# Attention's constants loaded during layer norm, the one-hot products turned round, and late projections stored by ScalarE's queue

## The chip, the cores and the metric

The kernel runs on one core of a Trainium2 chip. A core has five engines that work at the same time, each through its own instructions in order: PE (TensorE, matrix products into PSUM), DVE (VectorE), ACT (ScalarE), POOL (GpSimd) and SP (SyncE, which here only issues DMAs). DMAs are issued from the queues of SP, ACT and POOL and are carried out by 16 DMA engines that all three share. An engine stands still while its next instruction waits for a semaphore, whatever is queued behind that instruction.

The metric is the device time of one execution in microseconds. One execution has been profiled as well; times below are counted from the start of its span.

## What is computed

The input x has 2 x 2048 tokens of 256 numbers. Cut to what matters:

```python
xn = (x - mean(x)) / sqrt(var(x) + 1e-5)              # layer norm
q, k, v = xn @ W.T + b                                # 16 heads of 16
rpk, rpv = rel_k[idx], rel_v[idx]                     # idx = clip(key - query, -128, 128) + 128
w = softmax((q @ k.T + q . rpk) / 4)
s = ((w @ v + w . rpv) as rows) @ Wo.T + bo           # attention with relative positions
e = argmax(xn @ Wg + bg)                              # one of 8 experts for a token
g = silu(gelu(xn @ W1[e]) @ W2[e])                    # 256 -> 1024 -> 256
out = x + s * g
```

All of it is float32.

## The kernel before, in words

The work is done in stages, one behind the other on PE.

**Layer norm, up to about 58 us.** Eight blocks of 512 tokens. `take_stats(i)` takes the mean and variance of a block on DVE and the root on ACT; `normalise(i)` scales the block on DVE (`xn`, L249), stores it in `xn_d` by SP for the experts, and turns it on PE (`tps`, L259), ACT copying the result into `xnT`. `logits(i)` multiplies by Wg (`plog`, L267). The loop takes the statistics of block i + 1 before it normalises block i. Between the blocks, `work_pieces(n)` puts in the next n of a list of 28 pieces: query, key and value projections of the first half of the tokens (`queries`, `keys`, `right_rows`, `values_of`). Their results go to DRAM (`q_d`, `k_d`, `qx_d`, `v_d`) by SP. A piece `values_of` adds the bias to `vt` on DVE (L326); two tiles `vt`, preset to one by POOL (L390), are used in turn.

**Routing, from 58 to about 125 us.** DVE counts the tokens of each expert by one-hot tables and gives every token a slot in a list in which each expert's tokens fill whole tiles of 256. To turn the list round (which token is in which slot), 32 matrix products add up over blocks of 128 tokens: `atplace` (128 x 128, one-hot of the place in a block of slots) and `inblock` (128 x 46, the token's number at its block of slots) give `ptok` (128 places x 46 blocks), copied to `token`. In the profile each float32 product is two passes, so these are 64. POOL then gathers the tokens of the first two tiles (`get_tokens`), SP loads the weights of their experts (`get_weights`: a value load of the expert's number, then W1 and W2, 1 MB each), and POOL loads attention's constants: `wo_t`, `bo_t`, `relk_t`, `rvd`, `rvc`, `ones_r`. DVE presets the key tiles `kT` from `ones_r` (L542) and builds `into` from `rvc` (L546); PE multiplies `into` by each group of `wo_t` and DVE adds that to `wo_t` (L551, L554), here called the fold. The last value pieces stand around this.

**Experts, from 125 to about 397 us.** 19 tiles of 256 tokens (`work`): PE turns the tokens (`xp`), multiplies by W1 (`hp`), ACT takes gelu, PE multiplies by W2 (`yp`), and the result is stored by ACT's queue (`ys_d`).

**Attention, from 397 us to the end.** 128 chunks: a loop over n takes a chunk of 128 queries of four heads. Its scores against nearby keys, the band, take a way of their own: `rel_scores` (L855) and `to_keys` send the relative scores through DRAM (`qr_d`, then back as `r`) on SP; `band_scores` (L893) adds them; `band_weights` takes exponentials on ACT (L926) and sends the weights through DRAM (`w_d`, back as `wr`) on POOL. Four chunks make a unit, whose far keys are taken by `far_scores` (L1048, exponentials L1058) and `far_values` (L1068). Each n has about five steps; the functions put down by `at(k, ...)` are issued behind step k. Within these, the first four n also do the query, key and value projections of the second half of the tokens, which `load_late` prepares: it loads the weights, the bias `bvl` and the turned tokens `sacc` (from `xT_d`) by ACT's queue and adds a constant to `bvl` on DVE (L711). `late_rows` (L729, L735), `late_right` (L744) and `late_values` (L759, L767) are these pieces. Each stores its result by SP at once; the pool of the late `vt` tiles has two buffers, preset by POOL (L754).

The order in each of the stages is written out by hand. Instructions of a later stage can nevertheless stand between those of an earlier one in an engine's queue: POOL's first memsets of L754 run at 88.6 us.

Of the kernel before, what the change touches and what calls it, by code (L numbers as in the profile page):

```python
# [34 lines left out]
def attn_moe_gate_kernel(  # L35
# [137 lines left out]
    with ExitStack() as own:  # L173
# [172 lines left out]
        def work_pieces(n):  # L346
            for what, *args in pieces[:n]:
                what(*args)
            del pieces[:n]

        take_stats(0)
        for i in range(NI):
            if i + 6 < NI:
                get_x(i + 6)
            if i + 1 < NI:
                take_stats(i + 1)
            normalise(i)
            if i == 0:
                nc.vector.tensor_scalar(bq_t, bq_t, HD**-0.5, None, ALU.mult)
                nc.vector.tensor_scalar(bk_t, bk_t, rkc[:, 0:1], None, ALU.add)  # L360

                nc.vector.tensor_tensor(
                    right, rkc[:, 1:2].to_broadcast([P, HEADS]),
                    rkc[:, 0:1].to_broadcast([P, HEADS]), ALU.subtract,
                )
# [15 lines left out]
                nc.gpsimd.memset(ones, 1.0)  # L381
                nc.gpsimd.memset(zq, 0.0)
                nc.gpsimd.iota(
                    begin, pattern=[[TE, NE]], base=0, channel_multiplier=0,
                    allow_small_or_imprecise_dtypes=True,
                )
                nc.gpsimd.iota(place, pattern=[[1, P]], base=0, channel_multiplier=0)
                nc.gpsimd.iota(number, pattern=[[P, NT]], base=0, channel_multiplier=1)
                for vt in vts:
                    nc.gpsimd.memset(vt, 1.0)  # L390
                for n in range(NI):
                    nc.sync.dma_start(out=qx_heads[:, 0, n * TB : (n + 1) * TB], in_=zq)
            if i == 1:
                nc.vector.tensor_tensor(
                    bvl, bvl, rve[:, 0:1, :].to_broadcast([P, HEADS, HD]), ALU.add
                )
            if i > 0:
                logits(i - 1)
                work_pieces(1)
            if i > NL:  # L400
                n = i - 1 - NL
                nc.sync.dma_start(
                    out=xT_d[n * P : (n + 1) * P, :].rearrange("p (k t) -> p k t", k=ND),
                    in_=xnT[:, :, (i - 1) * TB : i * TB],
                )
        logits(NI - 1)
        work_pieces(1)
        nc.sync.dma_start(
# [83 lines left out]
        ptok = lnps.tile([P, NB], F32, name="tps")  # L492
        for i in range(NI):
            ts = slice(i * CB, (i + 1) * CB)
            nc.vector.tensor_tensor(
# [14 lines left out]
        nc.vector.tensor_reduce(expf, over, AX.X, ALU.add)  # L510
        nc.vector.tensor_scalar(expert, expf[:, :, 0], float(E - 1), None, ALU.min)
        nc.vector.tensor_copy(filled, ends[:, E - 1 : E])
        work_pieces(13)
        for t in range(NT):
            nc.tensor.matmul(
                ptok, lhsT=atplace[:, t, :], rhs=inblock[:, t, :], start=(t == 0),
                stop=(t == NT - 1),
            )
        nc.vector.tensor_copy(token, ptok)
        inputs = [get_tokens(i, feed) for i in range(2)]  # L520
        weights = [get_weights(i, feed) for i in range(2)]


        wo_t = load("wo_t", [P, NG, D], wo.rearrange("(g p) m -> p g m", p=P))
        bo_t = load("bo_t", [P, D], bo.partition_broadcast(P))
        relk_t = load("relk_t", [P, TB], relk)
        rvd = load("rvd", [P, 2, HD], relv.rearrange("(a p) d -> p a d", p=P))
        rvc = load("rvc", [P, 2], relv_cols)
        ones_r = load("ones_r", [P, 1], ones_rows)
        nc.gpsimd.memset(zeros, 0.0)  # L530
        into = tables.tile([P, HG, 32], F32, name="into")
        nc.gpsimd.memset(into, 0.0)
        for t in q_homes:
            nc.gpsimd.memset(t, 0.0)
        nc.gpsimd.memset(stat, LOW)
# [2 lines left out]
        for z in shifts:  # L538
            nc.gpsimd.memset(z, 0.0)
        work_pieces(len(pieces) - 2)  # L540
        for t in k_homes:
            nc.vector.tensor_copy(t, ones_r.to_broadcast([P, S]))  # L542

        nc.vector.tensor_tensor(vdiff, rvc[:, 1:2], rvc[:, 0:1], ALU.subtract)
        for j in range(HG):
            nc.vector.tensor_copy(  # L546
                into[32 * j : 32 * j + 32, j, MASS : MASS + 1], vdiff[32 * j : 32 * j + 32, :]
            )
        for g in range(NG):
            ps = lnps.tile([P, D], F32, name="tps")  # L550
            nc.tensor.matmul(  # L551
                ps, lhsT=into.rearrange("p j i -> p (j i)"), rhs=wo_t[:, g, :], start=True, stop=True
            )
            nc.vector.tensor_tensor(wo_t[:, g, :], ps, wo_t[:, g, :], ALU.add)  # L554

        nc.vector.tensor_copy(rel0, relk_t[:, 0:1])
        nc.vector.tensor_scalar(relk_t, relk_t, rel0, None, ALU.subtract)
        nc.vector.tensor_tensor(rvd, rvd, rve[:, 0:1, :].to_broadcast([P, 2, HD]), ALU.subtract)
# [86 lines left out]
    def _attention(own, again):  # L645
# [59 lines left out]
        def load_late():  # L705
            tiles = [outp.tile([P, ND, D], F32, name=n) for n in ("gt", "gt", "xo", "xo")]
            for t, w in zip(tiles, (wq, wk, wv)):
                nc.scalar.dma_start(out=t, in_=w.rearrange("(k p) m -> p k m", p=P))
            bvl = tiles[3][:, 0, :].rearrange("p (h x) -> p h x", x=HD)
            nc.scalar.dma_start(out=bvl, in_=bv.partition_broadcast(P))  # L710
            nc.vector.tensor_tensor(  # L711
                bvl, bvl, rve[:, 0:1, :].to_broadcast([P, HEADS, HD]), ALU.add
            )
# [7 lines left out]
            late["w"], late["bvl"], late["xT"] = tiles[:3], bvl, xT  # L721

        def late_rows(i, n, a):

# [8 lines left out]
            t = exps.tile([P, TB], F32, name="ex")  # L733
            bias, scale, dst = ((bq_t, HD**-0.5, q_d), (bk_t, 1.0, k_d))[n]
            nc.scalar.activation(t, ps, AF.Identity, bias=bias[:, a : a + 1], scale=scale)  # L735
            nc.sync.dma_start(out=dst[a * P : (a + 1) * P, cols], in_=t)
            if n == 0:
                lateq[i, a] = t

        def late_right(i):  # L740
            cols = slice((NL + i) * TB, (NL + i + 1) * TB)
            ps = sps.tile([P, TB], F32, name="sp")
            for a in range(ND):
                nc.tensor.matmul(  # L744
                    ps[:HEADS, :], lhsT=rights[a], rhs=lateq.pop((i, a)), start=(a == 0),
                    stop=(a == ND - 1),
                )
            rt = exps.tile([P, TB], F32, name="ex")
            nc.scalar.copy(rt[:HEADS, :], ps[:HEADS, :])
            nc.sync.dma_start(out=qx_heads[:, 1, cols], in_=rt[:HEADS, :])  # L750

        def late_values(i, half):
            vt = vtp.tile([P, NG, 2, HG, VW], F32, name="vt")
            nc.gpsimd.memset(vt, 1.0)  # L754
            ps = sps.tile([P, 2, NG, HG, HD], F32, name="sp")
            for c in range(2):
                t0 = (2 * half + c) * P
# [8 lines left out]
            for c in range(2):  # L766
# [3 lines left out]
                    late["bvl"].rearrange("p (g j) x -> p g j x", j=HG),  # L770
                    ALU.add,
                )
            w = HG * VW
            n = NL + i
            nc.sync.dma_start(
                out=v_d[n * P : (n + 1) * P, :].rearrange("p (g c w) -> p g c w", c=CB, w=w)[
                    :, :, 2 * half : 2 * half + 2, :
                ],
                in_=vt.rearrange("p g c j x -> p g c (j x)"),
            )  # L780

        late_pieces = []
        for i in range(NI - NL):
# [413 lines left out]
        while n < NCH or values or any(queues) or n <= NCH + 2 * CB + 1:  # L1197
# [180 lines left out]
```

## Time and profile before

| what | value |
|---|---|
| time, median of 3 runs | 2311.96 us (2306.64 to 2318.05) |
| the profiled execution's own time | 2312.8 us |
| its span, first to last instruction | 2311.1 us |
| PE busy | 2205.3 us (95%) |
| ACT busy | 1295.6 us (56%) |
| DVE busy | 1063.1 us (46%) |
| POOL busy | 443.2 us (19%) |
| moved by DMA | 488.31 MB, mean 211 GB/s |
| layer norm and routing, until the experts' first turn | 0 to 124.7 us |
| experts | 124.7 to 396.9 us |
| attention | 396.9 us to the end |

How to read the rows. A row of the timeline or of a group has the engine, the line of the kernel, the operation, what it writes and reads, their shapes and the count; in the timeline the start and the time from first to last end stand ahead, and in square brackets the idle time of that engine before it and what ended it. PEld is PE's loading of weights, which overlaps its products. PEclk is the clock that PE was granted. A busy PE need not be PE at full speed, because its ends are modelled, so half clock shows in PEclk and in the duration of a pass rather than in the busy share. A window's row has the time that each engine was busy in a stretch, with its instructions, and after them the granted clock, the busy share of the 16 DMA engines and the rate.

### The profile page before, as it was taken

To read this page: it belongs to the slowest core of one execution; us is meant where nothing else is said; L and a number is where in the kernel's file an instruction comes from. 1 tells how busy PE (TensorE), PEld (TensorE's weight loads), DVE (VectorE), ACT (ScalarE), POOL (GpSimd) and SP (SyncE) were. 2 spreads that over 40 slices of the span, in tenths; PEclk is the share of its full clock that TensorE was granted. 3 is DMA by queue.
4 is the path that set the end of the run, shared out by engine and by line. 5 is a ranking of instruction groups with operands and counts; after the bars stand their busy time and mean duration, and the time that the engine had idled before them with its cause. 6 is when DMAs were issued, how large, how long until landed. Compare 5 with 4: busy or idle time off the path is not lost. (4 is left out here: it accounts for less than half of the span.)

```text
span 2311.1 us, 58525 instructions
## 1 busy us (share of the span) xinstructions
PE 2205.3 (95%) x24314; PEld 1432.7 (62%) x24314; DVE 1063.1 (46%) x2689; ACT 1295.6 (56%) x2543; POOL 443.2 (19%) x643
## 2 busy tenths in 40 slices
PE   7899999899999999999999999999999999999997
PEld 5588887455666556656565555566666656566653
DVE  5410000245555455555455444455555555555542
ACT  2111111237777666767666566666666666666764
POOL 1211110011333333321111222211111111111221
PEclk9899999899999999999999999999999999999999
DMA  6565553677777667776676666666756676666652
GB/s 204 206 190 187 187 185 106 226 230 233 237 243 244 212 221 232 245 236 206 205 234 210 231 231 220 213 213 227 224 198 216 221 222 223 200 208 213 233 195 85
DMA packets 256534, 488.31 MB, mean 211 GB/s; under 512 B 17120, under 2 KB 204672, under 8 KB 255744
## 3 DMA queue, kind: packets, MB, share of 16 engines
q1 hardware_dynamic: 207840, 297.31, 39.6%
q0 software_dynamic: 41008, 178.84, 23.1%
q10 hardware_dynamic: 7408, 8.27, 1.1%
q8 instruction: 196, 3.21, 0.6%
q14 instruction: 82, 0.67, 0.1%
HBM read 247.91 MB, written 236.45 MB: 210 GB/s over the span
## 5 line engine op out<-in xcount | busy, mean ns | idle before, releaser
L1058 ACT ACTIVATE ex<-sp 128x512 f32<-128x512 f32 x1728 | 892.7, 587 | 535.7 <-PE sp L1048 412.4
L1048 PE MATMUL sp<-qh,kT 32*128 32x512 f32 (+7 forms) x4096 | 767.1, 560 | 19.3 <-DVE stat L903 19.2
L903 DVE CUSTOM_DVE_ANT_0 r<-sp,r 128x384 f32<-128x384 f32 (+1 forms) x512 | 275.5, 538 | 594.1 <-PE sp L1048 327.3
L893 PE MATMUL sp<-kT,qh 31*128 31x384 f32 (+1 forms) x1024 | 453.6, 523 | 0.0
L1048 PEld LDWEIGHTS sp<-qh,kT 31*128 31x128 f32 (+1 forms) x4096 | 298.0, 184 | 207.0 <-issue 136.1
L1068 PE MATMUL av<-ex,v 128*17 128x256 f32 (+2 forms) x7168 | 423.0, 371 | 0.0
L1068 PEld LDWEIGHTS av<-ex,v 128*17 128x17 f32 (+1 forms) x7168 | 195.3, 99 | 176.6 <-issue 69.0
L855 PE MATMUL sp<-relk_t,qh 32*128 32x256 f32 x1024 | 289.1, 404 | 12.0 <-DVE qr L864 9.4
L926 ACT ACTIVATE r<-r,shift 128x384 f32<-128x384 f32 (+1 forms) x512 | 283.2, 614 | 0.0
L969 DVE COPY wt<-mp 128x512 f32<-128x512 f32 x368 | 242.4, 684 | 11.2 <-PE mp L967 6.2
L967 PEld LDWEIGHTS mp<-ident,r 128*128 128x128 f32 x1472 | 156.3, 141 | 141.3 <-issue 130.2
L941 POOL DMA_DIRECT2D wr<-w_d x128 | 97.4, 761 | 704.6 <-PE sp L1048 168.4
L967 PE MATMUL mp<-ident,r 128*128 128x128 f32 x1472 | 217.0, 282 | 2.1 <-DVE wt L969 2.1
L864 DVE COPY qr<-sp 128x512 f32<-128x512 f32 x256 | 175.2, 685 | 41.9 <-PE sp L1048 32.6
L855 PEld LDWEIGHTS sp<-relk_t,qh 32*128 32x128 f32 x1024 | 169.9, 185 | 26.4 <-DVE qr L864 9.8
L990 PE MATMUL mp<-ident,wr 128*128 128x128 f32 x1024 | 158.1, 278 | 25.7 <-DMA wr<-w_d 15.2
L939 POOL DMA_DIRECT2D w_d<-r x128 | 72.7, 568 | 532.5 <-ACT r L926 525.2
L607 ACT ACTIVATE hT<-hp 128x512 f32<-128x512 f32 x76 | 45.3, 597 | 215.7 <-PE hp L600 215.7
L893 PEld LDWEIGHTS sp<-kT,qh 31*128 31x128 f32 x1024 | 150.4, 184 | 8.9 <-issue 5.7
L990 PEld LDWEIGHTS mp<-ident,wr 128*128 128x128 f32 x1024 | 120.3, 142 | 46.3 <-DVE qh L953 22.5
L600 PE MATMUL hp<-xsT,w_t 128*128 128x256 f32 x608 | 134.4, 379 | 1.0 <-DVE xsT L586 1.0
L615 PE MATMUL yp<-w_t,hT 128*128 128x256 f32 x608 | 134.4, 379 | 0.0
(189 smaller groups left out, 2023.9 us busy)
## 6 DMA issues: line engine op xcount, KB each, us to landing
qr_d<-qr SPq DMA_DIRECT2D x128, 768.0 KB
r<-qr_d SPq DMA_DIRECT2D x128, 768.0 KB
w_d<-r POOLq DMA_DIRECT2D x128, 768.0 KB, 5.0
wr<-w_d POOLq DMA_DIRECT2D x128, 512.0 KB, 4.4
w_t<-in_w_dram SPq DMA_DIRECT2D x38, 1024.0 KB
ys_d<-ys ACTq DMA_DIRECT2D x19, 256.0 KB
v<-v_d SPq DMA_DIRECT2D x32, 144.0 KB
xn_d<-xn SPq DMA_DIRECT2D x8, 512.0 KB
```

The costliest lines, as they stand in the source:

```text
L600: nc.tensor.matmul(ps[:, m, :], lhsT=w1_t[:, k, (h + m) * P : (h + m + 1) * P], rhs=xsT[:, k, :], start=(k == 0), stop=(k == ND - 1),)
L855: nc.tensor.matmul(ps[:, 2 * x * P : 2 * (x + 1) * P], lhsT=ch["un"]["q"][32 * j : 32 * j + 32, chunk(ch["i"] + x)], rhs=relk_t[32 * j : 3 ...
L864: nc.vector.tensor_copy(ch["qr"][:, :, j, : 2 * P], ps.rearrange("p (x r) -> p x r", x=2))
L893: nc.tensor.matmul(ps[:, :bw], lhsT=ch["un"]["q"][32 * j : 32 * j + RIGHT, chunk(ch["i"])], rhs=ch["gr"]["kT"][32 * j : 32 * j + RIGHT, ch ...
L903: nc.vector.tensor_tensor_reduce(out=r, in0=ps[:, :bw], in1=r, scale=1.0, scalar=LOW, op0=ALU.add, op1=ALU.max, accum_out=stat[:, n, j, 0:1],)
L926: nc.scalar.activation(r[:, j, f0 * P : f1 * P], r[:, j, f0 * P : f1 * P], AF.Exp, bias=shifts[n % (2 * CB)][:, j, ONE : ONE + 1],)
L967: nc.tensor.transpose(ps[:, x, :], ch["r"][:, j, chunk(f0 + f)], ident)
L969: nc.vector.tensor_copy(dst, ps)
L990: nc.tensor.transpose(ps[:, jj, a, :], ch["wr"][:, 2 * pair + jj, chunk(a)], ident)
L1048: nc.tensor.matmul(ps[:, at : at + e - a], lhsT=kT[32 * j : 32 * j + rows, chunk(kc)], rhs=q[32 * j : 32 * j + rows, a:e], start=True, sto ...
L1058: nc.scalar.activation(exs[j][:, :n], ps[:, :n], AF.Exp)
L1068: nc.tensor.matmul(un["av"][32 * j : 32 * j + cols, a:e], lhsT=v[:, kc, j, :cols], rhs=exs[j][:, at : at + e - a], start=False, stop=False ...
```

## The change

Three things are moved and one is turned round.

Layer norm: block 0 is normalised before the statistics of block 1 are taken. What followed the first block (scaling the biases, `rights`, tables of POOL) follows the second. The presetting of `vt` and the eight stores of zeros into `qx_d` follow the fifth. There a new function `set_up` issues the loads of attention's six constants by POOL and clears `into`, which both stood behind the token gathers.

Routing: the DVE work on these constants (`kT`, `vdiff`, `into`, `rel0`, `relk_t`, `rvd`) stands ahead of the 13 pieces. The products take `inblock` as the operand that is loaded into the array and `atplace` as the one that streams through it; the sum comes out as 46 x 128, is copied and turned. One value piece is worked between the copy and the turn.

Attention: the addition to `bvl` moves from `load_late` into the first `late_values`. The stores of late queries, keys and right rows are issued by ACT's queue instead of SP's. The stores of late values remain on SP and are issued behind the following step.

```diff
+        def set_up():
+            nc.gpsimd.dma_start(out=ones_r, in_=ones_rows)
+            nc.gpsimd.dma_start(out=rvc, in_=relv_cols)
+            nc.gpsimd.dma_start(out=wo_t, in_=wo.rearrange("(g p) m -> p g m", p=P))
+            nc.gpsimd.dma_start(out=bo_t, in_=bo.partition_broadcast(P))
+            nc.gpsimd.dma_start(out=relk_t, in_=relk)
+            nc.gpsimd.dma_start(out=rvd, in_=relv.rearrange("(a p) d -> p a d", p=P))
+            nc.gpsimd.memset(into, 0.0)
+
         take_stats(0)
         for i in range(NI):
             if i + 6 < NI:
                 get_x(i + 6)
-            if i + 1 < NI:
+            if i > 0 and i + 1 < NI:
                 take_stats(i + 1)
             normalise(i)
             if i == 0:
+                take_stats(1)
+            if i == 1:
                 nc.vector.tensor_scalar(bq_t, bq_t, HD**-0.5, None, ALU.mult)
...
-                for vt in vts:
-                    nc.gpsimd.memset(vt, 1.0)
-                for n in range(NI):
-                    nc.sync.dma_start(out=qx_heads[:, 0, n * TB : (n + 1) * TB], in_=zq)
-            if i == 1:
...
+            if i == 4:
+                for vt in vts:
+                    nc.gpsimd.memset(vt, 1.0)
+                for n in range(NI):
+                    nc.sync.dma_start(out=qx_heads[:, 0, n * TB : (n + 1) * TB], in_=zq)
+                set_up()
...
+        for t in k_homes:
+            nc.vector.tensor_copy(t, ones_r.to_broadcast([P, S]))
+
+        nc.vector.tensor_tensor(vdiff, rvc[:, 1:2], rvc[:, 0:1], ALU.subtract)
...
         work_pieces(13)
+
         for t in range(NT):
             nc.tensor.matmul(
-                ptok, lhsT=atplace[:, t, :], rhs=inblock[:, t, :], start=(t == 0),
+                ptok[:NB, :], lhsT=inblock[:, t, :], rhs=atplace[:, t, :], start=(t == 0),
                 stop=(t == NT - 1),
             )
-        nc.vector.tensor_copy(token, ptok)
+        tokb = ln1.tile([P, P], F32, name="tokb")
+        nc.vector.tensor_copy(tokb[:NB, :], ptok[:NB, :])
+        work_pieces(1)
+        ps = lnps.tile([P, NB], F32, name="tps")
+        nc.tensor.transpose(ps, tokb[:NB, :], ident[:NB, :NB])
+        nc.vector.tensor_copy(token, ps)
         inputs = [get_tokens(i, feed) for i in range(2)]
         weights = [get_weights(i, feed) for i in range(2)]
-
-
-        wo_t = load("wo_t", [P, NG, D], wo.rearrange("(g p) m -> p g m", p=P))
...
-        for t in k_homes:
-            nc.vector.tensor_copy(t, ones_r.to_broadcast([P, S]))
...
-            nc.vector.tensor_tensor(
-                bvl, bvl, rve[:, 0:1, :].to_broadcast([P, HEADS, HD]), ALU.add
-            )
...
-            nc.sync.dma_start(out=dst[a * P : (a + 1) * P, cols], in_=t)
+            nc.scalar.dma_start(out=dst[a * P : (a + 1) * P, cols], in_=t)
...
-            nc.sync.dma_start(out=qx_heads[:, 1, cols], in_=rt[:HEADS, :])
+            nc.scalar.dma_start(out=qx_heads[:, 1, cols], in_=rt[:HEADS, :])
...
+            if (i, half) == (0, 0):
+                nc.vector.tensor_tensor(
+                    late["bvl"], late["bvl"], rve[:, 0:1, :].to_broadcast([P, HEADS, HD]), ALU.add
+                )
...
+            late["v"].append((i, half, vt))
+
+        def store_values():
...
+                    at(k + 1, store_values)
```

More of the change, by code (lines that the diff above doesn't have):

```diff
@@ L349, in work_pieces @@
             del pieces[:n]
+        wo_t = const.tile([P, NG, D], F32, name="wo_t")
+        bo_t = const.tile([P, D], F32, name="bo_t")
+        relk_t = const.tile([P, TB], F32, name="relk_t")
+        rvd = const.tile([P, 2, HD], F32, name="rvd")
+        rvc = ln1.tile([P, 2], F32, name="rvc")
+        ones_r = ln1.tile([P, 1], F32, name="ones_r")
+        into = ln1.tile([P, HG, 32], F32, name="into")
+        def set_up():
[6 more added lines that the diff above has]
+            nc.gpsimd.memset(into, 0.0)
         take_stats(0)
@@ L491, in attn_moe_gate_kernel @@
         atplace = tables.tile([P, NT, P], F32, name="atplace")
-        ptok = lnps.tile([P, NB], F32, name="tps")
+        ptok = lnps.tile([P, P], F32, name="tps")
         for i in range(NI):
@@ L512, in attn_moe_gate_kernel @@
         nc.vector.tensor_copy(filled, ends[:, E - 1 : E])
+        for t in k_homes:
+            nc.vector.tensor_copy(t, ones_r.to_broadcast([P, S]))
+        nc.vector.tensor_tensor(vdiff, rvc[:, 1:2], rvc[:, 0:1], ALU.subtract)
+        for j in range(HG):
+            nc.vector.tensor_copy(
+                into[32 * j : 32 * j + 32, j, MASS : MASS + 1], vdiff[32 * j : 32 * j + 32, :]
+            )
+        nc.vector.tensor_copy(rel0, relk_t[:, 0:1])
+        nc.vector.tensor_scalar(relk_t, relk_t, rel0, None, ALU.subtract)
+        nc.vector.tensor_tensor(rvd, rvd, rve[:, 0:1, :].to_broadcast([P, 2, HD]), ALU.subtract)
         work_pieces(13)
@@ L515, in attn_moe_gate_kernel @@
             nc.tensor.matmul(
-                ptok, lhsT=atplace[:, t, :], rhs=inblock[:, t, :], start=(t == 0),
+                ptok[:NB, :], lhsT=inblock[:, t, :], rhs=atplace[:, t, :], start=(t == 0),
                 stop=(t == NT - 1),
             )
-        nc.vector.tensor_copy(token, ptok)
+        tokb = ln1.tile([P, P], F32, name="tokb")
[4 more added lines that the diff above has]
+        nc.vector.tensor_copy(token, ps)
         inputs = [get_tokens(i, feed) for i in range(2)]
         weights = [get_weights(i, feed) for i in range(2)]
-        wo_t = load("wo_t", [P, NG, D], wo.rearrange("(g p) m -> p g m", p=P))
[L525 to L529, printed above, removed]
         nc.gpsimd.memset(zeros, 0.0)
-        into = tables.tile([P, HG, 32], F32, name="into")
-        nc.gpsimd.memset(into, 0.0)
         for t in q_homes:
@@ L540, in attn_moe_gate_kernel @@
         work_pieces(len(pieces) - 2)
-        for t in k_homes:
[L542 to L547, printed above, removed]
-            )
         for g in range(NG):
@@ L554, in attn_moe_gate_kernel @@
             nc.vector.tensor_tensor(wo_t[:, g, :], ps, wo_t[:, g, :], ALU.add)
-        nc.vector.tensor_copy(rel0, relk_t[:, 0:1])
-        nc.vector.tensor_scalar(relk_t, relk_t, rel0, None, ALU.subtract)
-        nc.vector.tensor_tensor(rvd, rvd, rve[:, 0:1, :].to_broadcast([P, 2, HD]), ALU.subtract)
         work_pieces(len(pieces))
@@ L710, in load_late @@
             nc.scalar.dma_start(out=bvl, in_=bv.partition_broadcast(P))
-            nc.vector.tensor_tensor(
-                bvl, bvl, rve[:, 0:1, :].to_broadcast([P, HEADS, HD]), ALU.add
-            )
             xT = accp.tile([P, NC, D], F32, name="sacc").rearrange("p c d -> p (c d)")
@@ L720, in load_late @@
                 )
-            late["w"], late["bvl"], late["xT"] = tiles[:3], bvl, xT
+            late["w"], late["bvl"], late["xT"], late["v"] = tiles[:3], bvl, xT, []
         def late_rows(i, n, a):
@@ L754, in late_values @@
             nc.gpsimd.memset(vt, 1.0)
+            if (i, half) == (0, 0):
+                nc.vector.tensor_tensor(
+                    late["bvl"], late["bvl"], rve[:, 0:1, :].to_broadcast([P, HEADS, HD]), ALU.add
+                )
             ps = sps.tile([P, 2, NG, HG, HD], F32, name="sp")
@@ L772, in late_values @@
                 )
+            late["v"].append((i, half, vt))
+        def store_values():
             w = HG * VW
[L774 to L780, printed above, removed]
+            for i, half, vt in late["v"]:
+                n = NL + i
+                nc.sync.dma_start(
+                    out=v_d[n * P : (n + 1) * P, :].rearrange("p (g c w) -> p g c w", c=CB, w=w)[
+                        :, :, 2 * half : 2 * half + 2, :
+                    ],
+                    in_=vt.rearrange("p g c j x -> p g c (j x)"),
+                )
+            late["v"] = []
         late_pieces = []
```

## The prediction

> **What bounds the kernel now.** I read the page's first two parts, then PE's timeline up to 130 us and from 395 to 500, then waits and windows there.
>
> ```profile
> PE 2205.3 (95%) x24314; PEld 1432.7 (62%) x24314; DVE 1063.1 (46%) x2689; ACT 1295.6 (56%) x2543; POOL 443.2 (19%) x643
> PEclk9899999899999999999999999999999999999999
> ```
>
> PE is the bound. Only a hole in its timeline, or a stretch at half clock, can be won. Both lie where this change works: slices 2 and 8 of PEclk fall below 9. The windows of the routing stage (columns: length, then PE, PEld, DVE, ACT and POOL busy with counts, clock, DMA share, GB/s):
>
> ```profile
> 87.80:91.20 3.40, 3.40 (x33) 3.37 (x31) 0.76 (x2) 0.00 (x0) 1.10 (x2) 1.00 0.61 180
> 91.20:98.30 7.10, 7.10 (x36) 7.10 (x35) 0.00 (x0) 0.00 (x0) 0.00 (x0) 0.50 1.05 385
> 105.30:116.90 11.60, 0.00 (x0) 0.00 (x0) 3.76 (x9) 0.00 (x0) 6.54 (x20) 0.63 0.55 158
> ```
>
> PE runs the one-hot products first at full clock, then at half, although it never pauses, and later stands still for 11.6 us. The timeline says what is around this:
>
> ```profile
> 87.86 10.64 PE L515 MATMUL tps<-inblock,atplace 128*128 128x46 f32 x64
> 98.29 6.99 PE L318 MATMUL pp<-wv_t,xnT 128*128 128x256 f32 x24
> 116.98 3.75 PE L551 MATMUL tps<-wo_t,into 128*128 128x256 f32 x8 [11.70 <-DVE into L546]
> 120.53 4.32 PE L318 MATMUL pp<-wv_t,xnT 128*128 128x256 f32 x16
> 124.69 0.60 PE L582 MATMUL xp<-ident,xs 128*128 128x128 f32 x4
> 113.57 2.36 DVE L542 COPY kT<-ones_r 128x2048 f32<-128x2048 f32 x2 [7.50 <-DMA ones_r<-in_ones_rows_dram]
> ```
>
> The stall is a chain: POOL issues the loads of attention's constants behind the token gathers, `ones_r` last; DVE waits for it, fills `kT`, builds `into`; PE waits for `into`. After 124.69 the experts keep PE busy for 271.2 of 272.2 us, so their start shifts whole. In layer norm:
>
> ```profile
> 11.11 1.38 DVE L249 TENSOR_SCALAR xn<-xt,mv,rs 128x256 f32<-128x256 f32 x4
> 15.01 3.38 DVE L249 TENSOR_SCALAR xn<-xt,mv,rs 128x256 f32<-128x256 f32 x4
> 15.24 2.04 POOL L390 MEMSET vt<- 128x1152 f32 x2
> 17.49 2.29 PE L259 MATMUL tps<-ident,xn 128*128 128x128 f32 x8 [3.61 <-DVE xn L249]
> ```
>
> PE waits for block 1; its normalisation takes 3.38 instead of 1.38 us while POOL clears `vt`. At the start of attention:
>
> ```profile
> 409.97 0.43 DVE L711 TENSOR_TENSOR xo<-xo,rve 128x256 f32<-128x256 f32 x1 [12.32 <-DMA xo<-in_bv_dram]
> 410.31 2.48 DVE L864 COPY qr<-sp 128x512 f32<-128x512 f32 x4
> 411.05 2.07 PE L855 MATMUL sp<-relk_t,qh 32*128 32x256 f32 x4 [9.40 <-DVE qr L864]
> 413.05 1.22 PE L729 MATMUL sp<-sacc,gt 128*128 128x512 f32 x1
> ```
>
> DVE holds four finished drains behind an addition whose operand is still loading.
>
> **Layer norm.** Block 0 is normalised before block 1's statistics: xn(0) at about 6.4 (root done at 6.1) instead of 11.11. This alone gains little, because PE's unbroken work begins with block 1, which follows the statistics of block 2. DVE began those at 12.69 without a wait, so the data was there by then; they take 2.1, the reciprocal 0.2, so xn(1) starts at 14.7 to 15.0, as now. The gain is the memset that no longer lies across it: 2.0 us. From 23 to 48.6 PE is 100% busy, so that shift lasts.
>
> [...] But POOL is in order and the memsets, though written at block 4, wait for nothing there: POOL reaches them right after its tables, which now hang on `right` at about 16.6, so near 19 to 21, across xn(2). [...] I take -2; ends +1 and -4.
>
> Moved along: six POOL loads (0.6 to 0.8 us of issue each, about 0.9 MB together) and a 0.28 us memset, over a DMA share of 0.56 where nothing more is awaited; eight `zq` stores on SP (6.0 us there) that now stand before xn_d(5) and later stores, which nobody awaits before the gathers at 99. DVE's moved work (`kT` 2.36, `vdiff` and `into` 0.8, `relk_t` and `rvd` 0.8: 4.0 us) falls into its idle 5.3 us before 88.13, beside PE's projections. All zero; without that cover 4 us.
>
> **One-hot products.** 64 passes stay 64. At full clock about 30 fit in 3.34 us, 0.11 each; at half clock 34 take 7.3, 0.21 each. After the swap, 46 columns are loaded and 128 stream. A row for 128 streamed columns is L259: 8 in 1.04 us, 0.13 with its lead-in; L283 streams 512 in 0.49, so 128 in 0.12. [...] What it can win is the clock: the passes that lose it stream 46 columns per 0.11 us, an array mostly idle; 128 streamed columns look like the transposes and projections that keep 1.00 from 58.5 to 87.8. I take 64 x 0.112 = 7.2 (-3.2); ends -4 (0.10 each) and +3 (half clock throughout, 13.6). The three value groups behind it run at 1.8 instead of 2.33 (-1.5).
>
> Added: a DVE copy (0.2, beside a value group moved up), two passes of transpose (0.25) and the token cast behind that group's additions. The token comes 10.2 us after the products begin, instead of 10.9. First gather 0.3 later, second +1.3, landing 4.6 after: tile 0's tokens at 16 to 17. But value group (1, 1) now stores `v_d` on SP ahead of `get_weights`: those four loads, issued at 87.86 under the products until now, go out at about 11.3. W1 of tile 0 needs about 5 (at 180 GB/s until 91.2 and 385 after it, its 1 MB is there by 92.5 to 93), so 16.5; W2 20.5.
>
> **The stall.** PE's row from the products on becomes: 7.2 + 1.8 + 0.25 + 3.6 (two groups) + 1.8 (the fold, eight passes of 0.224, warm) + 3.6 = 18.3, then xp and at 20 the first expert product. Before: 124.69 - 87.86 = 36.8. That is -18.5, from start to start: stall 11.7, products 10.4 to 7.2, value groups and fold 14.7 to 10.8, transpose +0.25. Tokens have 1.5 us of room, weights 3.5.
>
> **Start of attention.** DVE drains at about 400 instead of 410.3, so `qr_d` and `r` go 9 us earlier. PE then meets the next lateness: L729 needs `sacc` (4 x 512 KB issued from 403.3). At the 200 to 230 GB/s of these slices it arrives at 411 to 413, later if `qr` shares the bandwidth; PE began L729 at 413.05. So 0 to -3 of the 9.4: I take -2. `store_values` takes eight `v_d` stores out from before `qr_d` on SP; the gap between DVE's copy and `qr_d` was about 2 us once, with no PE wait behind it: zero.
>
> The 20 late stores move to ScalarE: each 0.37 us (the `ys_d` row), plus a wait for its own activation that now blocks ACT. Behind them stand the band exponentials L926, then POOL's `w_d`, `wr`, `vt` memset, then DVE, then PE (0.4 us at 453, 2.1 at 491). ACT is busy 21.4 of 75.7 us, so all but two or three are covered: +1. Ends: 0 and +8 (all 20 x 0.4).
>
> **Sum.** -2 - 18.5 - 2 + 1 = -21.5. The profiled execution took 2312.8 (span 2311.1), 0.8 above the median of 2311.96. So 2291.
>
> **Rivals.** *Stall only*: the clock drops in the products as before, and attention gives nothing; about -13, 2299. [...] *Weights late*: the four loads behind `v_d` miss the experts by 3 to 5 us; 2295. Against it: 3.5 us of room. *ScalarE's queue blocks* (slower): SP's issues are often held (six loads in 11.17 us in layer norm, two `k_d` in 3.95). If ACT's stores are held the same way, 1.9 us each, 20 of them delay exponentials by 38 us; with PE's slack of 3 us, +35 - 20 = 2327. It decides above 1.2 us per store. Against it: ScalarE's queue carries little and its own issues took 0.37 to 0.50. *It doesn't do what it says*: queues hold other stages' instructions (a late `vt` memset stood on POOL before the gathers, waiting 71 us); one placed before a gather or load could undo the gain: 2312.
>
> **How the numbers follow.** Half a per cent, 11.6 us, is about what a measurement here tells from no change. As forecast 0.60 (2283 to 2297), stall only 0.14, weights late 0.08, undone 0.08, blocked queue 0.10. Stall only lies at the border and gives a little to "same". Range 2280 to 2306; chances 0.80, 0.10, 0.10.
>
> **What would show it.** Right: no PE gap over 1 us between products and xp; products at 7 to 8 us with clock 1.00; xp near 104; no wait of DVE for `bv`, and PE waiting for `sacc` at attention's start instead. Wrong: products over 10 us; PE waiting for `w_t`; ACT's DMA rows over 1 us; L926 later relative to attention's start.

## The result and the profile after

| | before | after |
|---|---|---|
| time, median of 20 runs each | 2309.88 us (2296.75 to 2322.93) | 2289.87 us (2279.93 to 2309.37) |
| the profiled execution's own time | 2312.8 us | 2289.33 us |
| its span | 2311.1 us | 2287.6 us |
| mean granted clock of PE in it | 0.974 | 0.980 |

The ratio is 0.9915, 95% interval 0.9894 to 0.9936: faster by 0.85%, 20 us, where 21.5 had been forecast (2291). The interval spans gains of 15 to 24 us. It confirms the one large step of the forecast; that the median came within 2 us of the sum is partly luck, because the small steps are below what it can tell. Two rows from the first parts of the page after:

```profile
PE 2196.7 (96%) x24315; PEld 1427.7 (62%) x24315; DVE 1063.1 (46%) x2690; ACT 1296.2 (57%) x2543; POOL 442.6 (19%) x643
PEclk9999998999999999999999999999999999999998
```

PE stays the bound. Slice 2 of PEclk, which was at 8 (the routing), is at 9 now; the first slice below 9 is slice 7, which holds the start of attention. The windows of layer norm's slow stretch, the products, and what follows them up to the experts (length; PE, PEld, DVE, ACT and POOL busy with counts; clock, DMA share, GB/s):

```profile
50.40:57.30 6.90, 6.90 (x28) 6.36 (x28) 0.00 (x0) 1.17 (x2) 0.00 (x0) 0.51 0.28 96
88.70:96.00 7.30, 7.30 (x66) 7.03 (x65) 0.76 (x2) 0.00 (x0) 0.00 (x0) 1.00 0.01 3
96.00:107.00 11.00, 11.00 (x50) 9.14 (x51) 4.84 (x14) 0.00 (x0) 6.95 (x12) 1.00 0.65 222
```

The products run at 1.00, and the 11 us behind them hold 11.00 us of PE. The timeline of the same stretch, and DVE's first row of the moved work:

```profile
88.78 7.19 PE L549 MATMUL tps<-atplace,inblock 128*46 128x128 f32 x64
95.90 1.99 PE L318 MATMUL pp<-wv_t,xnT 128*128 128x256 f32 x8
97.83 0.26 PE L557 MATMUL tps<-ident,tokb 46*128 46x46 f32 x1
98.02 3.72 PE L318 MATMUL pp<-wv_t,xnT 128*128 128x256 f32 x16
101.57 2.04 PE L572 MATMUL tps<-wo_t,into 128*128 128x256 f32 x8
106.91 0.60 PE L599 MATMUL xp<-ident,xs 128*128 128x128 f32 x4
83.60 2.35 DVE L535 COPY kT<-ones_r 128x2048 f32<-128x2048 f32 x2
```

No row has a bracket: the wait of 11.70 us for `into` is gone, `kT` is filled at 83.60 instead of 113.57, and the experts begin at 106.91 instead of 124.69. At the start of attention the wait of 9.40 us behind `bv` has become another (PE's timeline, then PE's waits from 375 to 525 us: total, times, longest):

```profile
393.74 6.10 PE L743 MATMUL sp<-sacc,gt 128*128 128x512 f32 x8 [7.27 <-DMA sacc<-xT_d]
...
PE mp L990 <- DVE wt L992: 3.2, 1, 3.2
PE sp L743 <- DVE vt L785: 0.8, 1, 0.8
```

Between the same marks of both profiled executions:

| stretch | before | after | difference | forecast |
|---|---|---|---|---|
| start of the span to the products | 87.86 | 88.78 | +0.9 | -2 |
| products to the experts' `xp` | 36.83 | 18.13 | -18.7 | -18.5 |
| `xp` to the experts' end | 272.2 | 272.2 | 0 | 0 |
| experts' end to the first attended product (`av`) | 112.10 | 111.95 | -0.15 | -1 |
| from there to the end | 1802.1 | 1796.5 | -5.6 | 0 |
| span | 2311.1 | 2287.6 | -23.5 | -21.5 |

In this pair of executions the large step came out right and the small ones did not. Much of the small ones is the executions' own, as the other runs show below. The experiments take the parts one by one.

### The profile page after: what moved, and what is told of

The parts are those of the page before. It is cut to its first block, busy times and chain, and to the rows that moved or that the text cites. A ratio compares the mean times of both kernels' runs of the same rounds, so it can differ in the third digit from the quotient of the medians.

```text
span 2287.6 us, 58518 instructions
## 1 busy us (share of the span) xinstructions
PE 2196.7 (96%) x24315; PEld 1427.7 (62%) x24315; DVE 1063.1 (46%) x2690; ACT 1296.2 (57%) x2543; POOL 442.6 (19%) x643
## 3 DMA queue, kind: packets, MB, share of 16 engines
q0 software_dynamic: 41008, 178.84, 23.5%
```

## The experiments

"Products to xp" and the other marks are those of the table above. Ratios are to the kernel before as it ran on the same occasion, with 95% intervals; medians of different rows come from different occasions and are not to be compared with each other. The last three columns are of one profiled execution each. The first attended product is the first product of far weights with values (`far_values`).

| run | median us | ratio | products at | products to xp | experts' end to first av |
|---|---|---|---|---|---|
| before | 2309.88 | 1 | 87.86 | 36.83 | 112.10 |
| after | 2289.87 | 0.9915 (0.9894 to 0.9936) | 88.78 | 18.13 | 111.95 |
| constants alone | 2285.16 | 0.9918 (0.9893 to 0.9943) | 87.14 | 20.97 | 111.82 |
| products alone | 2310.14 | 1.0024 (0.9998 to 1.0051) | 88.26 | 37.41 | 111.15 |
| attention alone | 2306.35 | 0.9997 (0.9978 to 1.0016) | 96.72 | 34.70 | 110.30 |
| layer norm alone | 2308.32 | 1.0004 (0.9986 to 1.0021) | 86.58 | 36.60 | 111.36 |
| products, 128 columns streamed | 2290.78 | 0.9923 (0.9888 to 0.9959) | 86.85 | 17.66 | 110.25 |
| late stores on SP (one run) | 2289.55 | | 89.22 | 18.12 | 111.84 |
| late loads reordered | 2279.73 | 0.9884 (0.9844 to 0.9923) | 88.91 | 18.12 | 105.15 |
| early presets, as first built | 2295.74 | 0.9947 (0.9922 to 0.9971) | 85.11 | 18.11 | 111.33 |
| early presets | 2277.09 | 0.9866 (0.9807 to 0.9924) | 89.10 | 18.12 | 102.52 |
| loads and presets | 2272.12 | 0.9843 (0.9810 to 0.9875) | 86.27 | 18.12 | 97.81 |
| loads and presets, again | 2281.92 | 0.9865 (0.9815 to 0.9914) | 87.20 | 18.12 | 97.54 |
| loads, presets, 128 columns | 2280.65 | 0.9887 (0.9852 to 0.9923) | 86.20 | 17.66 | 97.98 |

**The constants alone.** The kernel before with `set_up` behind block 4 of layer norm and the DVE work on the constants ahead of the 13 pieces:

```diff
+            if i == 4:
+                set_up()
...
+        for t in k_homes:
+            nc.vector.tensor_copy(t, ones_r.to_broadcast([P, S]))
...
         work_pieces(13)
```

> The kernel before with one part: attention's constants are loaded during layer norm and DVE's work on them stands ahead of the 13 pieces. Theory (the stall was the chain POOL loads, ones_r, kT, into): the 11.7 us gap of PE before the fold goes, and with it the half clock of fold and value groups; from the start of the one-hot products to the experts' first turn 10.4 + 7.0 + 1.8 + 3.6 = 22.8 us instead of 36.8, so -14. The products stay at 10.4 with half clock in their second part. Rival (the parts add up one by one, each by its own share): the gap alone, -11.7.

The stall is gone, and products to `xp` falls by 15.9 us. This part alone carries the whole gain that can be measured. Its products keep the old form; PE's row and the windows from their start to the drop of the clock and from there to their end:

```profile
87.14 8.76 PE L545 MATMUL tps<-inblock,atplace 128*128 128x46 f32 x64
...
87.10:92.60 5.50, 5.50 (x51) 5.47 (x50) 0.75 (x2) 0.00 (x0) 1.10 (x2) 1.00 0.79 259
92.60:96.00 3.40, 3.40 (x17) 3.40 (x17) 0.06 (x1) 0.00 (x0) 0.00 (x0) 0.50 1.08 387
```

The clock still falls, 5.5 us after the products begin, and is back 6.8 us later. In before it fell a second time, at 108.3 in the stall; with no stall there is no second fall, and the fold and the value groups behind it take 2.4 us less. With the 11.7 us of waiting that makes 14, as the theory had it. The other 1.9 us are in the products, because the clock fell later here than in before, 5.5 us after their start instead of 3.4. That is the execution's own and no merit of the edit. In the clock's records of all fourteen traces it changes only on a grid of steps of 3.41 us, which lies elsewhere in each execution. In the four kernels that stream 46 columns it fell after 3.4, 5.5, 4.4 and 3.4 us (before, constants, attention and layer norm alone), each time at the end of the first step that the products filled, to within 0.04 us.

**The products alone.** The kernel before with the operands exchanged, the copy, the turn and the value piece between:

```diff
-                ptok, lhsT=atplace[:, t, :], rhs=inblock[:, t, :], start=(t == 0),
+                ptok[:NB, :], lhsT=inblock[:, t, :], rhs=atplace[:, t, :], start=(t == 0),
...
+        work_pieces(1)
+        ps = lnps.tile([P, NB], F32, name="tps")
+        nc.tensor.transpose(ps, tokb[:NB, :], ident[:NB, :NB])
+        nc.vector.tensor_copy(token, ps)
```

> The kernel before with one part: the products take the narrow table as the loaded operand. Theory: products 7.2 us at clock 1.00, but behind them PE waits for the constants, which hang on the token; the token comes about 1 us earlier, so the experts start only about 1 us earlier: -1, and the gain of 3.2 turns into a longer stall (about 14 us). Rival (the parts add up): -3 to -5 in the whole time.

The products take 7.19 us at clock 1.00, as in after, and nothing comes of it. DVE's and PE's timeline, and the window of the stall:

```profile
115.64 2.36 DVE L547 COPY kT<-ones_r 128x2048 f32<-128x2048 f32 x2 [13.63 <-DMA ones_r<-in_ones_rows_dram]
118.89 3.49 PE L556 MATMUL tps<-wo_t,into 128*128 128x256 f32 x8 [17.68 <-DVE into L551]
...
104.00:116.00 12.00, 0.00 (x0) 0.00 (x0) 0.36 (x1) 0.00 (x0) 7.38 (x22) 0.54 1.04 360
```

What PE gains it waits longer: 17.68 us instead of 11.70, where the theory had about 14. The wait grew by more than was won: `ones_r` now lands 9.1 us after its issue (106.52 to 115.64) instead of 6.6 (106.99 to 113.57). The value piece put between holds SP's queue at its `v_d` store (98.23), so the experts' 4 MB of weights go out from 99.37 instead of 87.9, beside the constants, and the DMA engines are at 1.04 through the stall, where they were at 0.55. That the load was slow for this reason is read from the trace; no run tests it apart.

**Attention alone**, with the later addition to `bvl`, the stores on ScalarE's queue and `store_values`:

```diff
-            nc.sync.dma_start(out=dst[a * P : (a + 1) * P, cols], in_=t)
+            nc.scalar.dma_start(out=dst[a * P : (a + 1) * P, cols], in_=t)
...
+                    at(k + 1, store_values)
```

> The kernel before with one part: all that the change does in attention (addition to bvl moved, late stores on ScalarE's queue, late value stores a step later). Theory (the 9.4 us wait for DVE turns into one for sacc; the rest of the difference in attention between the two profiles is the clock's own variation): from the end of the experts to the end of the first unit -1, whole time -1 within its uncertainty. Rival (the 5.7 us that attention was shorter in the profile after came from this part): -5 to -6.

```profile
416.38 6.45 PE L726 MATMUL sp<-sacc,gt 128*128 128x512 f32 x8 [7.40 <-DMA sacc<-xT_d]
```

The wait behind `bv` (9.40 us) has become this one for `sacc`. The first late product comes 12.73 us after the experts' end instead of 16.13, the first attended product 1.8 earlier; the total cannot be told from before. In this execution layer norm, whose code is that of before, had 17.1 us of half clock and ended 9 us later: a warning for the next reading.

**Layer norm alone**, with blocks 0 and 1 in the new order and the memsets and zero stores at block 4:

```diff
-            if i + 1 < NI:
+            if i > 0 and i + 1 < NI:
                 take_stats(i + 1)
             normalise(i)
             if i == 0:
+                take_stats(1)
+            if i == 1:
```

> The kernel before with one part: block 0 is normalised first, tables follow the second block, vt and the zeros the fifth. Theory (the turn of block 1 comes 1.8 us earlier, but where the clock's windows fall decides what is left): block 1 is turned at 15.7 instead of 17.5, and the products start between 86 and 89 us, at 87.9 in the mean: 0 within uncertainty. Rival (the order itself makes a later stretch of layer norm slower): products at 88.8, +1. Rival (the forecast's step): products at 86, -2.

PE turns block 1 at 16.18 instead of 17.49, and the products start 1.28 earlier; not measurable in the total.

**128 columns streamed.** Is it the narrow load that made the products cheap, or the 128 columns that stream? The kernel after with the wide table loaded again, but 128 columns streamed (the 46 of `inblock` and those behind them in memory, whose results nobody reads; POOL clears two more blocks of `inblock` for it); no turn, no second copy:

```diff
-                ptok[:NB, :], lhsT=inblock[:, t, :], rhs=atplace[:, t, :], start=(t == 0),
+                ptok, lhsT=atplace[:, t, :], rhs=flatin[:, t * NB : t * NB + P], start=(t == 0),
```

> The changed kernel with the products turned back (the wide table is the operand that is loaded, 128 columns), but each product streams 128 columns: the 46 of `inblock` and those that follow in memory. No transpose; the copy takes the first 46 columns. Theory 'a step costs what it streams and what it loads matters little': 64 products take about 7.2 us at a granted clock of 1.00, like the turned ones, and xp starts about 0.6 us earlier than in the changed kernel after the products' end, since transpose and second copy are gone: products' start to xp 17.0 to 18.2 us against 18.1. Theory 'a step costs its load of 128 columns, the narrow load was the gain': 8.8 to 10.6 us with part of it at half clock, as in before and in the run with the constants moved alone, and products' start to xp 19.5 to 21. Whole: within 2 us of the changed kernel (2290), not measurable, by either.

PE's timeline, then the window of the products:

```profile
86.85 7.31 PE L551 MATMUL tps<-inblock,atplace 128*128 128x128 f32 x64
...
86.80:94.20 7.40, 7.40 (x66) 7.36 (x66) 0.76 (x3) 0.00 (x0) 1.10 (x2) 1.00 0.86 290
```

With 82 useless columns in each product the clock stays at 1.00 and products to `xp` is 0.5 us shorter than in after. From start to start, one of the 64 passes takes 0.110 us at full clock in the old form (the 49 of the run with the constants alone), 0.110 in the new one and 0.112 here; at half clock the old form takes 0.213. So the exchange of the operands did not make a pass cheaper. What counts is that 128 columns stream: the clock stayed in all ten kernels whose products do that, and fell in all four whose products stream 46. Nor was it that the DMA engines stood idle beside the products of after (a share of 0.01): here they were busy (0.86), and the clock stayed.

**Late stores back on SP.** The kernel after with

```diff
-            nc.scalar.dma_start(out=dst[a * P : (a + 1) * P, cols], in_=t)
+            nc.sync.dma_start(out=dst[a * P : (a + 1) * P, cols], in_=t)
...
             late["v"].append((i, half, vt))
+            store_values()
```

> The changed kernel with the stores of the late projections and their values back on SP's queue, issued as in before; the constants, the turned products and the late add of the value bias stay. Theory 'the move of the stores is worth nothing by itself': first late product about 14.6 us after the experts' end, as in the changed kernel (7.3 us for sacc), and the first product of the attended values at +110.5 to +112.5, against +111.95. Rival 'ScalarE's stores give a lead that counts': +113 or more. Rival 'they cost a microsecond in the late stage, as the forecast had it': +111 or less.

The first late product comes at +13.06, earlier than the 14.6 expected, the wait for `sacc` is 5.7 us, and the first attended product at +111.84 against +111.95. By this mark the change of queue is worth nothing either way; the 1.5 us before it are won and lost again, and one execution can't tell them from chance.

**Late loads in another order.** The kernel after; ScalarE's queue loads wq, the first block of `xT`, then wk, wv and bv, and SP the other three blocks behind the first `r`:

```diff
             for t, w in zip(tiles, (wq, wk, wv)):
                 nc.scalar.dma_start(out=t, in_=w.rearrange("(k p) m -> p k m", p=P))
+                if w is wq:
+                    load_x(nc.scalar, 0)
...
+        if not again:
+            for x in range(1, NI - NL):
+                late["load"](nc.sync, x)
```

> The changed kernel with another order of the late stage's loads: wq, the first block of xT, then wk, wv and bv on ScalarE's queue; the other three blocks of xT on SP's, behind the load of the first row of r. Theory 'the first late product waits for data that come last of eight loads': the wait of 7.3 us for sacc falls to about 3, first late product at +10 to +11 from the experts' end (14.6), and the first r lands 4 to 8 us earlier since its store and load no longer share the DMA engines with all of the late loads; first product of the attended values at +107 to +109 (111.95); whole about 2286 to 2288 against 2290, ratio to before about 0.990. Rival 'the wait moves on': the second late block or the values wait for wk, wv or xT, and the first attended product stays at +111 to +112.

```profile
387.98 5.61 PE L748 MATMUL sp<-sacc,gt 128*128 128x512 f32 x8 [1.65 <-DVE av L1107]
```

The wait for `sacc` is gone. SP's rows of after, then of this run:

```profile
387.18 0.56 SPq L901 DMA_DIRECT2D qr_d<-qr  x1
399.28 0.40 SPq L903 DMA_DIRECT2D r<-qr_d  x1
```

```profile
387.04 0.57 SPq L906 DMA_DIRECT2D qr_d<-qr  x1
392.21 0.40 SPq L908 DMA_DIRECT2D r<-qr_d  x1
```

The row for `r` comes 5.2 us after that for `qr_d` (387.04 and 392.21) instead of 12.1 (387.18 and 399.28): in after, the relative scores had shared the DMA engines with all eight late loads. The first late product is at +8.72 and the first attended one at +105.15, earlier than the theory's 107 to 109; the median of 2279.73 is below its 2286 to 2288, too. The rival, that the wait moves on, is out. But the wait for `wt` stays, at 2.7 us.

**Early presets.** The kernel after; when a late value tile has been stored, POOL presets the next one at once instead of when it is used:

```diff
+        def preset():
+            late["made"] += 1
+            vt = vtp.tile([P, NG, 2, HG, VW], F32, name="vt")
+            nc.gpsimd.memset(vt, 1.0)
+            return vt
+
         def late_values(i, half):
-            vt = vtp.tile([P, NG, 2, HG, VW], F32, name="vt")
-            nc.gpsimd.memset(vt, 1.0)
+            vt = late["ready"].pop(0) if late["ready"] else preset()
...
+                if late["made"] < 2 * (NI - NL):
+                    late["ready"].append(preset())
```

A first build set up the list `ready` in a place that every late projection passes, so the tiles were preset and thrown away:

> The changed kernel with the early presets alone; the late loads keep their order. Theory 'the two waits are independent': the waits of 0.8 and 3.2 us for the adds behind the presets go, and the first attended product comes at +105 to +108 from the experts' end (111.95 in the changed kernel, 105.15 with the loads alone, 97.81 with both). Rival 'the preset counts only once the loads are early, because the rows of r hold the order of POOL and ScalarE': +110 to +112.

It decides nothing on the theory: POOL cleared six tiles more than in after, the one that is used next still stood behind `wr` (464.02), at 464.77, and PE's waits stayed (3.2 us for `wt`, 6.8 for `sacc`). With the list set up once:

> The changed kernel with the early presets alone, now with the list of preset tiles set up once (the run before emptied it at each late projection, so its tiles were preset and never used). [...] Rival 'early presets pay only with early loads': +109 or more.

POOL's timeline of after, then of this run:

```profile
469.10 0.76 POOL L964 DMA_DIRECT2D wr<-w_d  x1 [4.42 <-DMA w_d<-r]
469.84 1.11 POOL L768 MEMSET vt<- 128x576 f32 x2
```

```profile
455.87 0.58 POOL L770 MEMSET vt<- 128x576 f32 x1 [8.52 <-DMA v_d<-vt]
457.44 0.58 POOL L770 MEMSET vt<- 128x576 f32 x1 [0.99 <-DMA v_d<-vt]
467.62 0.76 POOL L972 DMA_DIRECT2D wr<-w_d  x1 [3.97 <-PE sp L783]
```

In after, the preset stands behind the load of `wr`, which waits for `w_d`; DVE's adds wait 7.3 us for it, `wt` stands behind them on DVE, and PE waits 3.2 us for `wt`. Here the preset is 10 us ahead of `wr`, and both waits are gone. The first attended product comes 9.4 us earlier, more than twice the 4.0 us of waits: in after a stretch of 10.2 us at half clock began at +94.6, 1.4 us behind the end of the 3.23 us wait, and this run has none there. Expected from two independent waits were +103 to +107; the rival, +109 or more, is out. It is no chance of two executions: ten of the fourteen kernels have this pause for `wt`, of 2.0 to 3.2 us, and in all ten a stretch of 6.8 to 13.7 us at half clock begins during it or within 3 us behind it; the four with early presets have neither. The pause of 2.1 us in before came with 6.8 us:

```profile
491.28 1.25 PE L967 MATMUL mp<-ident,r 128*128 128x128 f32 x8 [2.14 <-DVE wt L969]
```

Half clock between the experts' end and the first attended product was 27.3 us in after and 17.1 here.

**Both.**

> The run before this one (late loads in another order), and each value tile of the late stage is preset to ones by POOL right behind the preceding value stores instead of when it is used. Theory 'the late stage's products wait for POOL's preset, then for the adds behind it': the waits of PE for the value adds there, 0.8 and 3.2 us in the changed kernel, go, and the first attended product comes 2 to 4 us before that of the other run: +104 to +107. Rival 'these waits only hold what waits for the rows of r anyway': no difference to the other run within 1 us.

> The two edits of the late stage together, as run before (2272 us, ratio 0.984), on another occasion and beside the presets alone. Theory 'the gain is in the late stage and stays': first attended product at +97.5 to +98.5 from the experts' end, whole 2268 to 2280, ratio to before 0.982 to 0.988. Rival 'the earlier ratio was a lucky stretch of the attention's clock': ratio 0.990 or more, that of the changed kernel itself (0.9915).

PE's waits from 375 to 525 us in the second of the two, which are all that the view lists:

```profile
PE sp L891 <- ACTq L650: 2.0, 1, 2.0
PE sp L749 <- DVE av L1115: 1.6, 1, 1.6
PE sp L1084 <- DVE stat L939: 0.8, 1, 0.8
PE sp L891 <- issue: 0.4, 1, 0.4
PE sp L891 <- ACT ex L755: 0.2, 1, 0.2
```

The window from 379 to 500 us, of after and of this run:

```profile
379.00:500.00 121.00, 107.31 (x567) 57.30 (x570) 43.57 (x113) 36.35 (x64) 12.18 (x20) 0.89 0.67 221
```

```profile
379.00:500.00 121.00, 117.49 (x740) 63.35 (x741) 50.77 (x130) 45.68 (x81) 14.21 (x23) 0.96 0.77 253
```

PE is busy for 117.49 of the 121 us instead of 107.31, at a clock of 0.96 instead of 0.89. The first attended product comes at +97.81 and +97.54 instead of +111.95. For the first of the two the theory had +104 to +107: it counted the waits and not the half clock behind them. Both runs are faster than before; the first, with 0.9843 (0.9810 to 0.9875), is clear of the kernel after (0.9894 to 0.9936), the second, with 0.9865 (0.9815 to 0.9914), only by its middle. Its median of 2281.92 lies a little over what was expected, its ratio inside. The twelve runs of the two lie from 2262.73 to 2285.96, with a median of 2273.8.

**All three**, the two late edits and the 128 streamed columns:

> The two edits of the late stage (loads in another order, early presets) together with the products that stream 128 columns of the narrow table over the wide one as loaded operand. Theory 'each gain is in its own stage': products' start to xp 17.7 us (18.1 with the turned products), from experts' end to the first attended product about 98 us, whole about 2271 to 2273, ratio to before about 0.984, not to be told from the run with the turned products. Rival 'the value stores go ahead of the weights\' loads again or the gathers come late': a wait of PE before xp, 2 to 4 us more.

Products to `xp` and the late mark are as the theory had them; the total, 0.9887 (0.9852 to 0.9923), is not. Its six runs lie from 2267 to 2286, and no mark of its profiled execution (2267.11) explains the slower ones. That the 128 columns add anything to the other two is not shown.

## Why the prediction was right, and where not

**The stall (-18.5, measured -18.7).** Right in each term: stall 11.7 to nothing, products 10.64 to 7.19 (forecast 7.2), turn 0.26, value groups and fold at full clock. Tokens and weights were in time: `get_weights` went out at 99.89 behind `v_d`, and no wait for `w_t` shows, so *weights late* is out, in spite of the 12 us that they had moved back. The cover of DVE's moved work held: it ran from 83.60 to 87.4 beside PE's projections. What the sum hid is that its terms do not add: the constants alone bring 15.9 of the 18.7 and the products alone cost 0.6, yet on top of the constants they bring 2.8 (1.4 in the products, 1.4 in the value groups behind them). Without the late fall of the clock in that run it would be 14.0 and about 4.7, an estimate from the 1.9 us named there.

**The products' price.** The forecast took 0.112 us a pass, an estimate between the 0.11 of the 46 streamed columns in before and the 0.12 to 0.13 of its rows for 128, and looked for the gain in the clock. The runs bear out both: a pass takes 0.110 us with 46 columns loaded and 128 streamed, 0.110 with 128 loaded and 46 streamed at full clock, 0.112 with 128 of each, so that the narrower load made no pass cheaper, and with 128 streamed the clock stays at 1.00 over either load. That the array is mostly idle with 46 columns was the author's estimate of why the clock falls; the runs show that it falls, not why.

**Layer norm (-2, in the trace +0.9).** What this step said of the order of work on DVE and POOL held; what it left out is when PE's clock comes and goes. Block 1 is turned 1.76 us earlier, and the memset lies across `xn(2)` as forecast, which takes 3.17 us instead of 1.38, without a wait of PE:

```profile
15.73 2.30 PE L259 MATMUL tps<-ident,xn 128*128 128x128 f32 x8 [6.08 <-DVE xn L249]
19.49 3.17 DVE L249 TENSOR_SCALAR xn<-xt,mv,rs 128x256 f32<-128x256 f32 x4
19.51 2.04 POOL L423 MEMSET vt<- 128x1152 f32 x2
24.64 1.91 PE L259 MATMUL tps<-ident,xn 128*128 128x128 f32 x8
```

What the step missed is the last row. These transposes took 1.04 us in before, at full clock; here PE reaches them earlier, but the clock comes only at 26.60 (26.37 before), and half of the lead goes. A lead of 0.8 us is left at 30 us. Then one stretch at half clock is 6.8 us long instead of 3.4 (the first window shown above), and the products start 0.9 us later. That stretch follows a pause of PE which both kernels have; in after it reads:

```profile
49.36 2.01 PE L259 MATMUL tps<-ident,xn 128*128 128x128 f32 x8 [1.54 <-DVE xn L249]
```

All fourteen kernels have this pause of 1.54 us, and the same new order of blocks then loses 0, 3.4 or 6.8 us to half clock (one, five and four kernels). So, as far as these executions show, its length is not the order's doing. Over the kernels with one order or the other, at the same half clock before the products, the new order is ahead, in one execution of each: with 3.4 us of it they start at 86.2 to 87.2 (five kernels) against 87.9 and 88.3 (two), with none at 85.1 against 87.1. The gain of 1.4 to 2 us is there, but the clock's stretches, which were 0, 3.4, 6.8 and once 17.1 us long, are larger than it.

**Start of attention (-2 for the wait, +1 for ScalarE's stores; measured -0.15 together in this pair).** PE waits for `sacc` now, as forecast: the first late product comes 1.5 us earlier, inside 0 to -3. One pair of executions is too few for such sizes, but other kernels have the same code here. With the old code of attention (before, constants, products and layer norm alone) the first late product comes at +15.3 to +16.1, in the mean +15.7, and the first attended one at +111.2 to +112.1, in the mean +111.6. With the new code (after, attention alone, 128 columns) they come at +12.7 to +14.6, in the mean +13.9, and at +110.3 to +112.0, in the mean +110.8. So the lead at the start is 1.9 us and 0.8 of it is left, close to the -2 and -1 of the forecast, though the ranges of the later mark overlap.

So 1.1 us of the lead were lost again, about the forecast's +1, but the reason given for it is not the right one, and the size is luck. The stores cost ScalarE 0.33 us each and none of PE's waits there leads back to them: *ScalarE's queue blocks* is out. With the stores on SP the way from the first late to the first attended product is no shorter, 98.8 us against 97.3 in after. What grew instead are PE's waits behind the `vt` presets on POOL, from 0.4 to 0.8 and from 2.1 to 3.2 us, in a place that the sum had named only as cover, and half clock up to this mark, from 23.9 to 27.3 us. Why the waits grew is not shown. That the late loads, now level with the first `qr_d`, delay `r` is seen in the rows of SP above, but with these loads reordered the wait for `wt` was still 2.7 us. The runs with the loads and the presets show that these, not ScalarE's stores, hold the late stage: 14 us lay in them, the clock included.

**The rest of attention (0, in the trace -5.6).** Its code is the same. Over the fourteen profiled executions its length runs from 1789.6 to 1806.5 us, and the time at half clock within it from 35.4 to 69.5; a line through them has 0.44 us of length for each us at half clock (correlation 0.80). Before had 69.5 and after 56.0, so by this line about 6 of the 23.5 us between the two executions go with the clock and not with the change, an estimate that sets down all of the clock's difference to chance. The stretches ahead of it add up to 17.9; the medians differ by 20.0, and the interval does not tell the two apart. *Stall only* (2299) is out by its first sign, the clock in the products, and *it doesn't do what it says* by the missing bracket. The total could not have ruled *stall only* out: the constants alone, with the old products and the old attention, have the ratio of the whole change (0.9918 and 0.9915).

## What to carry over

When a load that everything waits for is issued behind work on which it does not depend, move it to where the queues have room: that alone was worth all that could be measured here, while a faster step ahead of the wait only made the wait longer (17.68 us instead of 11.70). After the wait is gone, list the next waits of PE in that stage and follow each back through the queues in which it stands: a memset of 1.1 us behind a load that waits held PE for 4 us and, through the clock, for 9. And before a saving of one or two us is read from two executions, compare their stretches at half clock.

## What the runs showed of the hardware

- PE's clock fell to half with no pause of PE in all four kernels whose products load 128 columns and stream 46, 3.4 to 5.5 us after their start; in all ten whose products stream 128, over either load, it stayed at 1.00.
- The clock changed only on a grid of steps of 3.41 us, so that a stretch at half clock is 3.4, 6.8, 10.2, 13.7 or 17.1 us long in all fourteen traces (but for the last, which the end of the trace cuts); where the grid lies differs between executions (the first change is at 26.37 us in before and at 26.60 in after).
- At half clock a pass that streams 46 columns over a load of 128 took nearly twice as long: 0.213 us against 0.110.
- A pause of 2.0 to 3.2 us in an otherwise busy stage came with 6.8 to 13.7 us at half clock in all ten kernels that have it; the four without the pause have no such stretch there. In after, where the waits came to 4.0 us, the run without them was 9.4 us ahead.
